# Moving ScalarE's copies and activations by half-states in a kernel of two interleaved layers

## The chip, the cores and the metric

The kernel runs on one core of a Trainium2 chip. The metric is the time in microseconds that the device takes for one launch. A core has a matrix engine (TensorE, here PE, with its weight loads shown as PEld), VectorE (DVE), ScalarE (ACT), GpSimd (POOL) and SyncE (SP), which here only issues transfers. Each engine works through its own queue in order, and they wait for each other through semaphores.

## The reference, cut to what matters

The input `x` is four images of 128 channels by 4096 positions, in fp32. Four layers follow each other; the change touches the first two.

Layer 0 is a selective scan over the positions of an image, with 256 inner channels and 16 states for each:

```python
xt = silu(causal_conv(in_proj(proj(x)))[:256])      # four taps; the other 256 outputs are zg
dt, Bm, Cm = split(xt @ x_proj_w.T)                 # 8 + 16 + 16
delta = softplus(dt @ dt_proj_w.T + dt_proj_b)
for t in positions:                                 # for each of the 16 states n
    h[n] = exp(delta[t] * A[n]) * h[n] + delta[t] * xt[t] * Bm[t, n]
    y[t] = sum_n h[n] * Cm[t, n]
x1 = out_proj((y + xt * D) * silu(zg)) + x
```

Layer 1 takes the group-normed `x1` and makes a hypergraph of the 4096 positions of each image:

```python
incidence = (distance(xf[i], xf[j]) < 16)           # 4096 x 4096 of 0 and 1, symmetric
xe = xf @ W_fc.T + b_fc
edge = (incidence.T @ xe) / degree
vert = (incidence @ edge) / degree
x2 = x1 + silu(batchnorm(vert + xf))
```

Layers 2 and 3 are a linear and a windowed attention, each with a sparse feed-forward layer. They stand in the last 790 us and are not touched.

## The kernel before, in words

**Two streams.** `layer0()` and `layer1()` are generators, and `layers01()` drives them side by side. Image 0 goes through layer 0 alone. Then, for each of the images 0, 1 and 2, layer 1 of image b runs beside layer 0 of image b+1: these are the shared rounds. Layer 1 of image 3 runs alone. Layer 1 of an image needs all of its x1, for the group norm and because every position is compared with every other.

**Layer 0.** An image is cut into eight chunks of T = 512 positions. A chunk takes 16 states, and a state two half-states (h = 0 and 1). A half-state is the unit of time of the whole schedule: one pass of the loop, one `tick`. Its number within a chunk is `u`, from 0 to 31. For each state, `rows` (L292) loads the two rows of B and C from memory on SP's queue, `drive` (L296) multiplies db on POOL, `state` makes two exponentials on ScalarE (L308) into a two-bank PSUM tile `hs` that has two buffers, two scans on VectorE (L314), and one product with C (L325). For image 0, six of the sixteen states have that product (L321) and the carry (L320) on POOL. For later images, POOL adds up groups of eight states instead (L330, L332). TensorE sums the terms (L353).

While one chunk is scanned, the next one is prepared. Its eleven steps are called at the half-states that `slots` names: load, project (eight products into two PSUM tiles `ps_c`, L234), conv (two SiLUs on ScalarE, L241), small (the products `ps_xd`, L247), rows_out (ScalarE's copy xd, L251, and the transfer of it to memory, L253, from which `rows` reads), delta (`ps_d`, L258), parts (L265, L266, twice), exp (L269), ln (L272), and inputs (dl and dx on POOL, L276 and L278). The current chunk's gate is `project_z` (`ps_z`, L361) at u = 9 and `gates` (two SiLUs, L366), and it is used at u = 6 of the following chunk (L371), after which L379 to L382 project, add and store x1.

**Layer 1.** `normed` and `squares` make xn and sq on ScalarE (L491, L486). `tokens` makes xe (products L504, sum on VectorE L508), which ScalarE copies to fp16 (`hi`, L511) and POOL subtracts for a second fp16 part (`lo`, L512). Then follow eight panels of 512 columns of the incidence, from the last to the first. A block is either compared (product L547, comparison on VectorE L550) or, where its mirror image exists, turned by TensorE (L559) and copied by ScalarE (L563). While a panel is made, the one before is multiplied with xs (`edges`, L570, reduced on VectorE L577, scaled and split by L581 to L588). Last comes, for each panel, a row of 1 / degree (`dg` on ScalarE L651, product `ps_r` L671, copied by ScalarE to `rb` L673), 64 products into `ps_v` (L678), and on VectorE the product of the two (`mean`, L686), which frees the bank under `ps_v`.

**What sets the order.** Each yield of `layer1` names its cost in nanoseconds of TensorE time as the writer estimated it; the driver asks for as many yields as keep the shares of both streams equal, about 330 for each half-state. `later(k, f)` puts off a call by k ticks. ScalarE's instructions are chained by hand in the order of the calls: `act()` makes each one follow the one before. For the other engines, the compiler's scheduler orders the instructions by its own cost model, so that a changed call moves instructions on all engines. All matrix products of both streams except `hs` share one PSUM pool, `ps`, of four banks.

Of the kernel before, what the change touches and what calls it, by code (L numbers as in the profile page):

```python
# [12 lines left out]
ALU = mybir.AluOpType  # L13
# [28 lines left out]
class Net:  # L42
# [36 lines left out]
    def layers01(self):  # L79
        nc, tc, a = self.nc, self.tc, self.a  # L80
# [10 lines left out]
        with ExitStack() as ctx:  # L91
# [93 lines left out]
            def follow(i, j):  # L185

                tc.add_manual_dep(
                    i.ins, j.name,
                    mybir.DependencyInfo(mybir.DependencyClass.NoSync, mybir.DependencyReason.DATA),
                    reason="order",  # L190
                )
# [4 lines left out]
            def act(i):  # L196


                if order:
                    follow(i, order[-1])  # L200
                order[:] = [i.ins]
# [5 lines left out]
            def later(k, f):  # L207
                waiting.append((self.tick + k, f))
# [76 lines left out]
            def rows(s, n):  # L285

                bcd = s["bcd"]
                bt = s["bt", n] = bcp.tile([P, 2, T], F32, tag="bt", name="bt")
                ap = bass.AP(
                    tensor=bcd.tensor, offset=bcd[n : n + 1, :].offset, ap=[[0, P], [DS * T, 2], [1, T]]  # L290
                )
                nc.sync.dma_start(bt, ap)  # L292

            def drive(s, n):
                db = s["db", n] = w2.tile([P, 2, T], F32, tag="db", name="db")
                nc.gpsimd.tensor_tensor(db, s["dx"], bc(s["bt", n][:, 0, :], 2), ALU.mult)  # L296
# [61 lines left out]
            def project_z(s):  # L358
                s["pz"] = [ps.tile([P, T], F32, tag="ps", name="ps_z") for h in range(2)]
                for h in range(2):  # L360
                    nc.tensor.matmul(s["pz"][h], wz[:, h, :], s["xt"][:, 3:], start=True, stop=True)  # L361

            def gates(s):
                zs = s["zs"] = late.tile([P, 2, T], F32, tag="zs", name="zs")
                for h in range(2):
                    act(nc.scalar.activation(zs[:, h, :], s["pz"][h], AF.Silu))  # L366

            def gate(s):

                for h in range(2):  # L370
                    nc.vector.tensor_tensor(s["xc"][:, h, :], s["y"][h], s["zs"][:, h, :], ALU.mult)  # L371

            def after(s):

                b, c, xc = s["b"], s["c"], s["xc"]
                x1 = w2.tile([P, T], F32, tag="x1", name="x1", bufs=1)
                po = ps.tile([P, T], F32, tag="ps", name="ps_o")
                for h in range(2):
                    nc.tensor.matmul(po, opT[:, h, :], xc[:, h, :], start=h == 0, stop=h == 1)  # L379
                nc.vector.tensor_tensor(x1, po, s["xt"][:, 3:], ALU.add)  # L380
                nc.vector.bn_stats(self.stats[:, b, c, :], x1)
                nc.scalar.dma_start(self.x1[b][:, c * T : (c + 1) * T], x1)  # L382

            def layer0():

                todo = [before(b, c) for b in range(B) for c in range(NT)]
                for f in todo[0][1]:
                    f()  # L390
                count = len(todo) * DS
                at = lambda i: (todo[i // DS][0], i % DS)

                slots = dict(zip((9, 14, 16, 18, 19, 20, 22, 23, 24, 25, 26), range(11)))

                def steps(k, u):

                    if k > 0:
                        if u == 6:
                            gate(todo[k - 1][0])  # L400
                        if u == 8:
                            after(todo[k - 1][0])
                    if k < len(todo):
                        if u == 9:
                            project_z(todo[k][0])
                        if u == 11:
                            gates(todo[k][0])
                    if k + 1 < len(todo) and u in slots:
                        todo[k + 1][1][slots[u]]()

                for i in range(3):
                    rows(*at(i))
                drive(*at(0))
                for i in range(count):
                    k, n = divmod(i, DS)
                    if i + 3 < count:
                        rows(*at(i + 3))
                    if i + 1 < count:
                        drive(*at(i + 1))
                    state(*at(i), 0)  # L420
                    steps(k, 2 * n)
                    yield
                    state(*at(i), 1)
                    if i > 2:
                        total(*at(i - 3))
                    steps(k, 2 * n + 1)
                    yield
                for i in range(count - 3, count):
                    total(*at(i))
                for u in (6, 8):  # L430
                    steps(len(todo), u)
                yield
# [42 lines left out]
            def layer1(b, rstd, nmr):  # L475
# [18 lines left out]
                def tokens(c, sq):  # L494

                    pc = ps.tile([P, CH], F32, tag="ps", name="ps_hc")
                    for v in range(4):
                        nc.tensor.matmul(
                            pc[:, v : v + 1], sq[:, v * P : (v + 1) * P], self.ones[:, 0:1], start=True, stop=True
                        )  # L500
                    nc.vector.tensor_scalar(hc[:, 4 * c : 4 * c + 4], pc[:, :4], 0.5, -HALF, ALU.mult, ALU.add)
                    pe = ps.tile([P, CH], F32, tag="ps", name="ps_e")
                    for v in range(4):
                        nc.tensor.matmul(  # L504
                            pe[:, v * P : (v + 1) * P], xn[c][:, v * P : (v + 1) * P], wT, start=True, stop=True
                        )
                    xe = tp.tile([P, 4, P], F32, tag="sq", name="xe")
                    nc.vector.tensor_tensor(xe, pe.rearrange("p (i c) -> p i c", c=P), bc(bfc, 4), ALU.add)  # L508
                    hi = xs[:, 4 * c : 4 * c + 4, 0:P]
                    lo = xs[:, 4 * c : 4 * c + 4, P + 1 : 2 * P + 1]  # L510
                    later(2, lambda: act(nc.scalar.copy(hi, xe)))  # L511
                    later(3, lambda: nc.gpsimd.tensor_tensor(lo, xe, hi, ALU.subtract))  # L512

                def row(c, sq=None):

# [144 lines left out]
                for c in range(NCH):  # L660
                    dg = ahead
                    if c < NCH - 1:
                        ahead = diagonals(c + 1)
                    inc = panels[c]
                    if c > 1:
                        inc = tp.tile([P, NB, CH], FP8, tag="inc", name="inc_v")
                        for q in range(4):
                            nc.sync.dma_start(inc[:, 8 * q : 8 * q + 8, :], panels[c][:, 8 * q : 8 * q + 8, :])

                    pr = ps.tile([P, CH], F32, tag="ps", name="ps_r")  # L670
                    nc.tensor.matmul(pr, self.ones, dg.rearrange("p i v -> p (i v)"), start=True, stop=True)  # L671
                    rb = tp.tile([P, CH], F32, tag="rb", name="rb")
                    later(1, lambda rb=rb, pr=pr: act(nc.scalar.copy(rb, pr)))  # L673
                    yield W_DEG
                    pv = ps.tile([P, CH], F32, tag="ps", name="ps_v")
                    for e in range(NB):
                        for k in range(2):
                            nc.tensor.matmul(  # L678
                                pv, es[:, e, k, :], inc[:, e, :],
                                start=e == 0 and k == 0, stop=e == NB - 1 and k == 1,  # L680
                            )
                        if e % 4 == 3:
                            yield W_VERT

                    def mean(c=c, rb=rb, pv=pv):
                        nc.vector.scalar_tensor_tensor(rb, pv, top, rb, ALU.mult, ALU.mult)  # L686
                        nc.gpsimd.tensor_tensor(rb, rb, xn[c], ALU.add)

                    def finish(c=c, rb=rb):

                        follow(nc.vector.bn_stats(stats[:, b, c, :], rb), scans[-1])
                        nc.sync.dma_start(self.hg[b][:, c * CH : (c + 1) * CH], rb)

                    due()
                    later(1, mean)
                    later(6, finish)
# [872 lines left out]
```

## Time and profile before

| | |
|---|---|
| median of three runs | 4049.89 us (4045.8 to 4050.37) |
| profiled execution, its own time | 4054.35 us |
| its span, first to last instruction | 4052.6 us |
| mean granted TensorE clock | 0.929 |
| busy, share of the span | PE 85%, DVE 74%, POOL 61%, ACT 50% |
| layer 0 of image 0 alone | 0 to 597 us |
| shared rounds | 597 to 1328, to 2070, to 2810 us |
| layer 1 of image 3 alone | 2810 to 3262 us |
| the rest of the network | 3262 to 4052 us |

In the lines of the profile, L is a line of the kernel, the arrow points from what is read to what is written, and the brackets at the end hold the idle time of the engine just before an instruction and what ended it. Idle time of an engine that is not the bottleneck costs nothing. The clock is the share of full speed that the throttle granted to TensorE.

### The profile page before, as it was taken

What the parts mean: (1) busy time and instruction counts of PE and PEld (TensorE: products, weight loads), DVE (VectorE), ACT (ScalarE), POOL (GpSimd) and SP (SyncE); (2) the same over time, 40 slices, a digit from 0 to 9 for tenths busy, and PEclk for the clock granted to TensorE, in tenths of its full rate; (3) what the DMA queues carried; (4) which work ended last, traced back from release to release, by engine and by line L of the source; (5) the groups of instructions that cost most, each with busy time, mean ns of one, the idle gap of its engine ahead of it and who ended that gap; (6) DMA issues with size and microseconds to landing.
All of it is one profiled execution on the core that took longest, in us unless ns stands there. A gap on an engine that the chain in (4) does not pass through costs nothing. (4 is left out here: it accounts for less than half of the span.)

```text
span 4052.6 us, 48609 instructions
## 1 busy us (share of the span) xinstructions
PE 3443.5 (85%) x17255; PEld 1930.0 (48%) x17255; DVE 2995.6 (74%) x4628; ACT 2035.6 (50%) x3364; POOL 2460.9 (61%) x1242
## 2 busy tenths in 40 slices
PE   6878768778889788888988888898999979998989
PEld 2333223344544334455433444544566457855864
DVE  5889889999767899976779998665641077665764
ACT  4556555445554545555544455642124068742951
POOL 5999989988779898976989888674000020001300
PEclk8889878999999889999987999998999989999999
DMA  3555544455437444543744555447121420045137
GB/s 103 149 145 156 151 123 127 132 134 156 121 115 233 114 138 131 142 141 91 228 140 128 135 139 150 112 148 242 55 74 49 141 90 12 12 163 200 28 116 296
DMA packets 263845, 532.71 MB, mean 131 GB/s; under 512 B 22794, under 2 KB 25266, under 8 KB 262578
## 3 DMA queue, kind: packets, MB, share of 16 engines
q1 hardware_dynamic: 255666, 519.09, 43.1%
q10 hardware_dynamic: 7936, 10.52, 0.8%
q8 instruction: 136, 2.23, 0.2%
q14 instruction: 107, 0.88, 0.1%
HBM read 451.80 MB, written 77.73 MB: 131 GB/s over the span
## 5 line engine op out<-in xcount | busy, mean ns | idle before, releaser
L296 POOL TENSOR_TENSOR db<-dx,bt 128x1024 f32<-128x1024 f32 x512 | 1203.9, 2355 | 291.2 <-DVE hs L314 159.7
L314 DVE TENSOR_TENSOR_SCAN hs<-hs,carry,db 128x512 f32<-128x512 f32 x812 | 1034.5, 1282 | 293.7 <-ACT hs L308 198.2
L308 ACT ACTIVATE hs<-dl,A 128x512 f32<-128x512 f32 x1024 | 705.9, 692 | 775.6 <-DVE ho L325 725.3
L547 PE MATMUL ps_g<-xn 128*128 128x512 f32 x1152 | 597.6, 646 | 120.6 <-DVE inc L550 86.3
L332 POOL TENSOR_TENSOR ho_s<-ho_s,ho 128x1024 f32<-128x1024 f32 x288 | 678.1, 2355 | 13.3 <-DVE ho L325 7.0
L325 DVE TENSOR_TENSOR ho<-hs,bt 128x1024 f32<-128x1024 f32 x464 | 563.1, 1214 | 1.5
L570 PE MATMUL ps_ed<-xs,inc 128*128 128x258 f16 x4096 | 511.6, 285 | 41.9 <-DVE inc L550 20.3
L570 PEld LDWEIGHTS <-inc 128*128 128x128 fp8e4 x4096 | 416.3, 102 | 160.2 <-issue 87.3
L550 DVE SCALAR_TENSOR_TENSOR inc<-ps_g,hcl,hb 128x512 fp8e4<-128x512 f32 x576 | 419.0, 735 | 32.3 <-PE ps_g L547 18.1
L547 PEld LDWEIGHTS ps_g<-xn 128*128 128x128 f32 x1152 | 210.9, 200 | 439.9 <-DVE inc L550 203.3
L563 ACT CAST inc<-ps_t 128x512 fp8e4<-128x512 f32 x448 | 231.8, 600 | 310.1 <-PE ps_t L559 282.6
L353 PE MATMUL ps_y<-ho,cst 128*128 128x512 f32 x512 | 275.3, 681 | 109.1 <-POOL ho L321 91.8
L678 PE MATMUL ps_v<-inc_v,es 128*128 128x512 fp8e4 x1536 | 344.0, 383 | 8.9 <-DVE rb L686 7.3
L678 PEld LDWEIGHTS <-es 128*128 128x128 f16 x2048 | 202.9, 99 | 277.2 <-issue 53.6
L234 PE MATMUL ps_c<-xt,wc 128*128 128x512 f32 x512 | 236.7, 617 | 2.7 <-DVE inc L550 2.1
L353 PEld LDWEIGHTS ps_y<-ho,cst 128*128 128x128 f32 x512 | 105.6, 215 | 269.7 <-POOL ho L321 122.1
L1238 POOL CAST b1h<-b 128x512 bf16<-128x512 f32 x2 | 1.4, 680 | 302.5 <-DMA b<-in_L_ffn_weight 302.5
L586 POOL TENSOR_TENSOR ed<-ed,rdeg 128x512 f32<-128x512 f32 x32 | 33.3, 1040 | 245.9 <-DVE rdeg L582 245.9
L314 DVE TENSOR_TENSOR_SCAN hs<-hs,db 128x512 f32<-128x512 f32 x116 | 141.3, 1224 | 49.4 <-POOL db L296 42.8
L577 DVE TENSOR_REDUCE ed<-ps_ed 128x129 f32<-128x258 f32 x128 | 52.9, 413 | 157.6 <-PE ps_ed L570 157.6
L234 PEld LDWEIGHTS ps_c<-xt,wc 128*128 128x128 f32 x512 | 100.5, 199 | 127.8 <-issue 116.1
L1474 POOL MEMSET ob<- 128x256 f32 x4 | 1.2, 312 | 261.7 <-PE ps_t L1417 261.7
(317 smaller groups left out, 5448.5 us busy)
## 6 DMA issues: line engine op xcount, KB each, us to landing
bt<-bcd SPq DMA_DIRECT2D x512, 512.0 KB, 5.0
w<-in_L_ffn_weight SPq DMA_DIRECT2D x64, 1024.0 KB, 11.4
inc<-inc SPq DMA_DIRECT2D x192, 256.0 KB, 2.3
inc_v<-inc SPq DMA_DIRECT2D x96, 512.0 KB, 6.3
strip<-inc SPq DMA_DIRECT2D x84, 256.0 KB, 2.9
x<-x ACTq DMA_DIRECT2D x32, 256.0 KB, 5.4
xn<-x SPq DMA_DIRECT2D x32, 256.0 KB, 6.2
hg<-rb SPq DMA_DIRECT2D x32, 256.0 KB, 2.5
```

The costliest lines, as they stand in the source:

```text
L234: nc.tensor.matmul(s["ps"][h], wc[:, h, j, :], xt[:, j : j + T], start=j == 0, stop=j == 3)
L296: nc.gpsimd.tensor_tensor(db, s["dx"], bc(s["bt", n][:, 0, :], 2), ALU.mult)
L308: act(nc.scalar.activation(hs[:, k, :], s["dl"][:, k, :], AF.Exp, scale=A[:, k, n : n + 1]))
L314: i = nc.vector.tensor_tensor_scan(to[:, h, :], hs[:, h, :], db[:, h, :], init, ALU.mult, ALU.add)
L325: nc.vector.tensor_tensor(ho, hs, ct, ALU.mult)
L332: nc.gpsimd.tensor_tensor(s["sum", n // G], s["sum", n // G], ho, ALU.add)
L353: nc.tensor.matmul(s["y"][h], self.ident, t[:, h, :], start=False, stop=n == DS - 1 and k == len(terms) - 1,)
L547: nc.tensor.matmul(pq, xn[v // 4][:, v % 4 * P : (v % 4 + 1) * P], xn[c], start=True, stop=True)
L550: nc.vector.scalar_tensor_tensor(inc[:, v, :], pq, hc[:, v : v + 1], hb, ALU.subtract, ALU.is_gt, saturate=False)
L563: later(1, lambda: act(nc.scalar.copy(inc[:, v, :], pt, saturate=False)))
L570: nc.tensor.matmul(pe[:, : 2 * P + 2], inc[:, v, i * P : (i + 1) * P], xs[:, v, :], start=v == 0, stop=v == NB - 1,)
L678: nc.tensor.matmul(pv, es[:, e, k, :], inc[:, e, :], start=e == 0 and k == 0, stop=e == NB - 1 and k == 1,)
```

## The change

Five places move. `slots` calls project one half-state earlier (14 to 13) and everything from rows_out on one half-state later, so that conv stands three half-states behind project instead of two, and rows_out two behind small instead of one; delta and the steps after it keep their distances. `gates` stands three half-states behind `project_z` instead of two. The copy of xe stands three ticks behind it instead of two, and POOL's subtraction goes one tick later with it. The copy of the row of 1 / degree stands three ticks behind its product instead of one.

```diff
@@ layer0
-                slots = dict(zip((9, 14, 16, 18, 19, 20, 22, 23, 24, 25, 26), range(11)))
+                slots = dict(zip((9, 13, 16, 18, 20, 21, 23, 24, 25, 26, 27), range(11)))
...
                         if u == 9:
                             project_z(todo[k][0])
-                        if u == 11:
+                        if u == 12:
                             gates(todo[k][0])
@@ layer1, tokens
-                    later(2, lambda: act(nc.scalar.copy(hi, xe)))
-                    later(3, lambda: nc.gpsimd.tensor_tensor(lo, xe, hi, ALU.subtract))
+                    later(3, lambda: act(nc.scalar.copy(hi, xe)))
+                    later(4, lambda: nc.gpsimd.tensor_tensor(lo, xe, hi, ALU.subtract))
@@ layer1, rows of 1 / degree
                     rb = tp.tile([P, CH], F32, tag="rb", name="rb")
-                    later(1, lambda rb=rb, pr=pr: act(nc.scalar.copy(rb, pr)))
+                    later(3, lambda rb=rb, pr=pr: act(nc.scalar.copy(rb, pr)))
```

## The prediction

> **What bounds the kernel now.** I read the page's table of engines first. It names no bound: PE 85%, DVE 74%, POOL 61% are means over unlike stages. So I asked for busy time by stretch. One shared round (layer 0 of image b+1 beside layer 1 of image b) is 597 to 1328 us; the rounds from 1328 and 2070 repeat it wait for wait.
>
> ```profile
> 0.00:597.00 597.00, 449.76 (x910) 182.50 (x911) 480.32 (x540) 335.47 (x445) 498.34 (x259) 0.87 0.48 138
> 597.00:1000.00 403.00, 329.19 (x1256) 163.93 (x1255) 379.79 (x486) 208.38 (x297) 361.13 (x164) 0.91 0.49 135
> 1000.00:1140.00 140.00, 116.47 (x775) 77.24 (x774) 100.51 (x124) 84.89 (x138) 100.26 (x46) 0.92 0.45 123
> 1140.00:1180.00 40.00, 31.95 (x163) 17.79 (x161) 20.74 (x26) 17.01 (x29) 21.23 (x12) 0.87 0.18 57
> 1180.00:1325.00 145.00, 140.26 (x562) 61.48 (x560) 108.73 (x117) 67.70 (x107) 132.78 (x61) 0.99 0.72 218
> ```
>
> After start and length the columns are busy us of PE, PE's weight loads, DVE, ACT, POOL, then granted TensorE clock. While panels are compared (597 to 1000) DVE is the bound: 379.79 of 403 us. While panels are mostly turned (1000 to 1140) nobody is above 84% and the engines wait for each other in order. From 1180 to 1325 PE is the bound (140.26 of 145), POOL next (132.78). In the first 597 us (layer 0 alone) it is POOL: 498.34 us busy, and half of its 99 us of idleness lies in the setup at the start.
>
> Next the waits of that round, since the change moves only what ScalarE waits for:
>
> ```profile
> DVE hs L314 <- ACT hs L308: 67.9, 21, 9.4
> ACT inc L563 <- PE ps_t L559: 50.1, 17, 5.9
> ...
> PE ps_g L547 <- DVE inc L550: 30.3, 32, 3.3
> ...
> ACT xd L251 <- PE ps_xd L247: 21.6, 8, 6.4
> ACT rb L673 <- PE ps_r L671: 20.9, 6, 10.3
> ...
> ACT xc L241 <- PE ps_c L234: 14.0, 4, 7.8
> ```
>
> Each line is a waiter, its releaser, us in all, times, longest. The change addresses xd, rb and xc: 56.5 us of ScalarE's waiting a round. What counts is the DVE idleness that they cause, part of the 67.9. In time order, 25 us of that 67.9 stands from 1000 to 1140 behind the turned panels' copies (L563), which stay where they are (one half-state behind); before 1000 only 9.2, also behind L563. The other 34 stands from 1140 on. On ScalarE's timeline, with what each waited for in brackets:
>
> ```profile
> 1144.17 0.69 ACT L241 ACTIVATE xc<-ps_c,vec 128x512 f32<-128x512 f32 x1 [7.80 <-PE ps_c L234]
> ...
> 1168.35 0.62 ACT L587 CAST es<-ed 128x512 f16<-128x512 f32 x1 [9.86 <-POOL ed L586]
> ...
> 1227.48 0.59 ACT L673 COPY rb<-ps_r 128x512 f32<-128x512 f32 x1 [10.29 <-PE ps_r L671]
> ```
>
> and on PE's, its one long gap there:
>
> ```profile
> 1170.20 2.07 PE L671 MATMUL ps_r<-dg,ones 128*128 128x512 f32 x2 [8.05 <-ACT dg L651]
> ```
>
> Between them xd (L251) waited 5.04 us until 1156.6. But there PE is the bound: DVE's gaps are mostly slack. Hence the gain is small.
>
> **The change part by part.** No instruction is added or removed but three activation table loads (227 against 224 in the built programs). Everything else is place in a queue. I compared the built instruction orders, which hold no times.
>
> Gates, xd, delta, parts, exp, ln and inputs move one half-state later; conv and small stay; the chunk's projection is asked for one half-state earlier, but on PE it stays within 3.5 us of its old place, so the 7.80 us wait at L241 stays. ACT's bcd DMA moves with xd; its reader, the bt load on SP, is issued six half-states later instead of seven, of about 2.9 us each (731 us / 256), and bt lands in 5.0 us: covered. If bcd were later than that, SP would hold every load behind it.
>
> *First stage.* The POOL order changes at each chunk end: the carry copy (L320) and ho (L321) come before dl (L276) instead of after.
>
> ```profile
> 219.98 2.34 POOL L276 TENSOR_TENSOR dl<-dl,sp 128x1024 f32<-128x1024 f32 x1 [0.42 <-ACT sp L272]
> ...
> 241.63 0.19 POOL L320 COPY carry<-ho 128x2 f32<-128x2 f32 x1 [0.61 <-DVE ho L314]
> ```
>
> ```profile
> 222.72 2.62 DVE L314 TENSOR_TENSOR_SCAN hs<-hs,carry,db 128x512 f32<-128x512 f32 x2 [2.71 <-POOL carry L320]
> ```
>
> DVE's 2.71 us goes, but POOL is the bound, so only POOL's own idleness counts: the 0.42 (dl starts 4.7 us later, after two 2.35 us operations, while ln is one half-state later) and about 0.3 of the 0.61: DVE starts the next chunk some 2 us earlier, but is then held by db, late next at 2.35 us each. 0.7 us by 8 chunks: -5.6. Bounds: 0, and -2 a chunk if DVE's lead were kept.
>
> *Compare and turn (597 to 1140), three times.* DVE has no gap behind an addressed wait here; what hides it is that ScalarE runs two states ahead. Gain 0. The cost is PSUM: ps has four banks; z and c keep two each for three half-states instead of two, xd one for two instead of one: 5 more bank-half-states of 128 in a chunk. DVE waited for PE's products about 17 us a round in all (inc 3.8, ed 9.8, hb 3.6). Bounds: 0, and +5 a round if these waits grow with the banks that layer 0 holds (about 16 to 21 of 128, +30%). Nearest row: inc's own 3.8, 30% of it 1.1. Taken: +1.3, +4 in all. Moving xe's copy and POOL's subtraction one half-state later shortens the time until xe's buffer is wanted (3.2 and 3.6 us at the tightest); xs waits are on ACT only. Counted at 0, bound +2 a round.
>
> A rule speaks against this step. The Trainium skill, "Perfetto Trace Analysis", section Identifying Performance Opportunities, says that the same bubble repeating on the engine that should be saturated can mean that no PSUM is free for the next tile. By that, PE's 30.3 us before ps_g, released by DVE, would grow by a third and cost up to +10 a round, +30. The rows differ: DVE, the bound, waits 3.8 us for these very products. I use the rows.
>
> Table loads: ACT_TABLE_LOAD is 1283 ns in the rows and the next instruction starts 10 to 20 ns later, so three cost 3.9 us. "ScalarE: Activation LUTs", What ACT_TABLE_LOAD costs, gives about 2.66 us per switch with its drain: 8 us. No row here shows that drain. ACT is busy 50%; counted 0.
>
> *End of the edges (1140 to 1180), three times.* Now: last edge product ends at 1160.2, ps_d follows (1.98), then PE idles 8.05 until dg. The last scans before the closing reduce (L577) start at 1158.6, because ScalarE stood at xd before the exps of that state. In the new order those exps come before xd: they can start at 1151.5, DVE's scans at 1155.3 instead of 1158.6. Reduce and reciprocal end near 1161.5, POOL's ho_s (2.34) and ed (1.04) near 1164.4, es and dg (0.62 + 1.26) near 1166.3. Late next is POOL. But ps_d now comes after ps_r, so PE idles 6.1 instead of 8.05: -1.9 a round, -5.8.
>
> *Products with the edges (1180 to 1325).* rb three half-states behind ps_r instead of one. ScalarE no longer stands 10.29 us at L673; PE had only 4.0 us of idleness in this stretch, 3.37 of it for DVE rb L686 freeing a bank. DVE runs ahead, POOL allows no more than its idleness. L686 stands one state (two scans of 1.28 and a product of 1.21, 3.8 us) later in DVE's order for five of the first seven panels. With DVE 5 us further ahead it comes out earlier: -2 in two rounds, -4. In the last stage (layer 1 alone) the same copy has 14 us of ps_v to hide in: 0.
>
> *Between rounds.* PE idles 7.25 us at 1325 for sq (L486) of the next image. In the new order the chunk projection (7.03 us) stands ahead of that wait. DVE only idles 0.97 + 1.23 for what this delays: -2 at two crossings, -4.
>
> Sum: -5.6 + 4 - 5.8 - 4 - 4 = -15.4. The profiled execution took 4054.35 us (span 4052.6 and 1.75 around it), so 4039; it is 0.11% above the median 4049.89, against which I forecast 4034.5.
>
> **The rivals.** A: no change (4042 to 4058). The waits only move: ScalarE stands at L563 instead, and PE decides. For it: DVE's gaps lie where PE is the bound. Against: the 0.42, the 8.05 and the order at the crossing. Time 4050, with the gains of the crossing and first stage eaten by PSUM.
>
> B: slower, by the bank under ps_v. A panel's bank is freed by L686, now a state later in DVE's order. Where PE comes to the next bank with none free it idles; it did 3.37 us once a round already. Three of the seven panel ends have no slack: PE waited for L686 at two (0.27 and 3.37), and at another ps_y's two banks were wanted 0.4 us after it. If DVE gains nothing, since POOL (132.78 of 145) holds it, each costs 3.6: 3 by 3.6 by 3 = +32. With the first stage (-5.6), the crossings (-4) and PSUM (+4), +27: 4077. With half of that, 4063. It decides once DVE is less than 3.6 us further ahead of PE at those ends.
>
> C: a larger gain: DVE's gaps at xc, xd, rb (6.64, 3.01, 5.67, 3.52, 3.46: 22.3 a round) are all worth time: -67, 3983. Against: PE busy 97% there.
>
> **How the numbers follow.** Forecast (faster by about 15) 0.5, A 0.2, B 0.25, C 0.05. The line between a change and none is 0.2%, 8 us, about what a measurement of this kernel tells apart. Faster 0.53, same 0.2, slower 0.27. The forecast's own range is 4020 to 4046. To hold 8 in 10 the range takes in A and most of B, 4012 to 4068.
>
> **What would show it.** Right: POOL's order at chunk ends without the 0.42; PE's gap before the first ps_r at 6 instead of 8.05; L673's wait for ps_r in shared rounds below 8 us in place of 20.9; ps_c in the gap at a round's start. Wrong: PE idle before ps_v in front of L686 for more than 5 us a round (B), more than 10 us of DVE waiting for ps_g a round (PSUM), or xe waiting for xs on POOL.

## The result: slower by 0.59%, and the profile after

The changed kernel took 4071.06 us (median of four runs, 4069.93 to 4074.56), the kernel before 4047.85 us on the same chip (four runs, 4042.37 to 4050.37). The ratio is 1.0059, 95% interval 1.0046 to 1.0072. The profiled execution of the changed kernel took 4071.98 us, its span is 4070.2 us, and the granted clock is 0.927 against 0.929. The clock is not what costs the time: the gates moved alone lose 17.8 us at a clock of 0.932. The forecast was 4034.5.

DVE's addition that makes x1 (L380, one a chunk) starts in the changed kernel 1.4 us earlier in chunk 0 of image 0, and then later by 1.9, 4.7, 8.7, 11.7, 14.3, 18.8 and 19.5 us. The last mean (L686) of the shared rounds is late by 19.3. So the loss has formed before the first shared round starts, and the three rounds together come out even. They do so because a gain and a loss meet in them: up to each round's first `ps_r` the three rounds together take 1779.4 us for 1799.7 before, and from there to the round's last mean 470.2 us for 450.1. (All figures of this kind are of one execution each. Where the instruction order is the same, two of them differ by some 3 us over the rounds.)

The first stage of the changed kernel (stretch, length, then busy us of PE, weight loads, DVE, ACT and POOL, then granted clock):

```profile
0.00:617.00 617.00, 459.66 (x933) 185.23 (x933) 482.38 (x541) 338.22 (x448) 495.97 (x259) 0.88 0.46 133
```

It is 20 us longer (617 for 597), while POOL, its bound, has the same work (495.97 for 498.34). The products with the edges in the first shared round, from the first `ps_r` to the last mean, before and after:

```profile
1170.20:1325.30 155.10, 150.30 (x596) 65.65 (x596) 114.33 (x123) 76.71 (x122) 135.77 (x62) 0.98 0.68 204
```

```profile
1183.00:1345.90 162.90, 153.39 (x601) 67.00 (x602) 114.99 (x122) 73.94 (x119) 135.78 (x62) 0.96 0.64 194
```

They are 7.8 us longer, and PE idles 9.5 us in them for 4.8.

**The first stage.** Between the first and the last x1 of image 0 lie seven chunks. Before:

```profile
126.00:558.50 432.50, 346.73 (x694) 136.49 (x692) 373.56 (x382) 257.74 (x342) 390.35 (x202) 0.89 0.52 150
```

After:

```profile
124.60:578.00 453.40, 353.01 (x693) 138.73 (x691) 375.06 (x383) 257.65 (x342) 390.37 (x202) 0.89 0.48 142
```

POOL is busy 390.35 and 390.37 us, so its idleness went from 42.15 to 63.03 us: 3.0 us a chunk more, which is the whole growth of the chunk (61.8 to 64.8 us). Now, who makes it wait? Waits of the same stretch, before (waiter, releaser, us in all, times, longest):

```profile
PE ps_y L353 <- POOL ho L321: 75.5, 23, 5.9
...
POOL carry L320 <- DVE ho L314: 27.2, 17, 4.0
...
DVE hs L314 <- POOL carry L320: 16.3, 6, 2.7
...
POOL dl L276 <- ACT sp L272: 3.8, 7, 1.2
```

And after:

```profile
PE ps_y L353 <- POOL ho L321: 95.4, 26, 6.1
POOL carry L320 <- DVE ho L314: 48.3, 22, 5.0
...
ACT xc L241 <- PE ps_c L234: 35.0, 14, 2.8
...
DVE ho L314 <- ACT hs L308: 26.9, 13, 4.3
```

The two waits that the prediction saw go have left the list: `dl` on `sp` and DVE on POOL's carry. Two others have grown from almost nothing: ScalarE waits 35.0 us for `ps_c` (1.5 before), and DVE 26.9 us for ScalarE's exponentials (0.5 before). POOL's wait for DVE grew by 21.1 us. On the timeline of the changed kernel one can follow the chain. PE:

```profile
264.73 3.61 PE L353 MATMUL ps_y<-ho,cst 128*128 128x512 f32 x4 [3.84 <-POOL ho L321]
268.18 7.03 PE L234 MATMUL ps_c<-xt,wc 128*128 128x512 f32 x16
```

ScalarE:

```profile
267.75 1.28 ACT L241 ACT_TABLE_LOAD   x1
271.81 0.69 ACT L241 ACTIVATE xc<-ps_c,vec 128x512 f32<-128x512 f32 x1 [2.78 <-PE ps_c L234]
275.25 0.69 ACT L241 ACTIVATE xc<-ps_c,vec 128x512 f32<-128x512 f32 x1 [2.75 <-PE ps_c L234]
275.95 1.28 ACT L308 ACT_TABLE_LOAD   x1
277.25 2.75 ACT L308 ACTIVATE hs<-dl,A 128x512 f32<-128x512 f32 x4
```

DVE, then POOL:

```profile
278.75 2.46 DVE L314 TENSOR_TENSOR_SCAN ho<-hs,carry,db 128x512 f32<-128x512 f32 x2 [4.22 <-ACT hs L308]
```

```profile
281.27 0.19 POOL L320 COPY carry<-ho 128x2 f32<-128x2 f32 x1 [4.91 <-DVE ho L314]
```

PE takes its queue in order. In front of `ps_c` now stand products of `ps_y` whose operand POOL makes, and PE waits 3.84 us for it. So `ps_c` starts late, ScalarE stands twice at `xc` with the table for SiLU loaded, the exponentials behind come late, DVE's scan with them, and POOL, the bound, idles 4.91 us. Before, the same chunk had on PE

```profile
255.29 1.88 PE L353 MATMUL ps_y<-ho,cst 128*128 128x512 f32 x4
257.00 7.03 PE L234 MATMUL ps_c<-xt,wc 128*128 128x512 f32 x16
263.87 2.31 PE L353 MATMUL ps_y<-ho,cst 128*128 128x512 f32 x5
```

with no wait, and ScalarE's two SiLUs ran at 264.14 without one. The gates are what put it there: between `ps_z` and the `ps_c` of chunks 2 to 7 of image 0, PE has four products of `ps_y` in every kernel below whose gates stay at u = 11 there, and eight in the change and in the kernel with the gates alone moved. The gates free the two banks of `ps_z`, and they come one half-state later. That the held banks are the scheduler's reason is a reading of the order; the place on PE is what the experiments below test.

**The shared rounds.** PE's gap before the first `ps_r` and its start of the next round, changed kernel:

```profile
1183.01 2.08 PE L671 MATMUL ps_r<-dg,ones 128*128 128x512 f32 x2 [6.01 <-ACT dg L651]
...
1345.74 7.03 PE L234 MATMUL ps_c<-xt,wc 128*128 128x512 f32 x16
1353.38 1.12 PE L520 MATMUL ps_hb<-sq,ones 128*128 128x512 f32 x2 [0.61 <-ACT sq L486]
```

The 8.05 became 6.01, and the 7.25 before `ps_hb` became 0.61, as forecast. ScalarE's wait for `ps_r`, 20.9 us in the first round, is down to

```profile
ACT rb L673 <- PE ps_r L671: 3.2, 3, 1.5
```

(The rounds do not repeat this wait as the prediction took it: 20.9, 11.5 and 41.6 us before, 3.2, 3.2 and 37.7 after.) But inside the edge products PE now waits:

```profile
1222.79 1.80 PE L678 MATMUL ps_v<-inc_v,es 128*128 128x512 fp8e4 x6 [2.27 <-DMA inc_v<-inc]
...
1326.94 8.36 PE L678 MATMUL ps_v<-inc_v,es 128*128 128x512 fp8e4 x32 [6.42 <-DMA bt<-bcd]
```

The first label is right. The product waits for a part of the third panel's incidence, which is loaded again from memory. On SP's queue that load stands behind the store of the first panel's result (`hg`, which SP holds until POOL has added to the mean) and behind a `bt` load for layer 0:

```profile
1214.16 0.33 SPq L692 DMA_DIRECT2D hg<-rb  x1
1214.59 0.39 SPq L292 DMA_DIRECT2D bt<-bcd  x1
1215.03 2.70 SPq L668 DMA_DIRECT2D inc_v<-inc  x3
```

The part landed at 1222.75, 7.7 us after its issue, and PE starts at 1222.79. Before, the load stood directly behind the store and landed after 4.4 us. The label of the second line is wrong, since that product reads no `bt`. DVE's timeline shows what it waits for:

```profile
1325.01 1.21 DVE L325 TENSOR_TENSOR ho<-hs,bt 128x1024 f32<-128x1024 f32 x1
1326.14 0.74 DVE L686 SCALAR_TENSOR_TENSOR rb<-ps_v,top,rb 128x512 f32<-128x512 f32 x1
```

DVE's mean, which frees the bank, ends at 1326.88 and PE starts at 1326.94. Before, the same gap bore DVE's name:

```profile
1305.88 2.41 PE L678 MATMUL ps_v<-inc_v,es 128*128 128x512 fp8e4 x7 [3.37 <-DVE rb L686]
```

The longer wait for the bank is rival B's mechanism in rival B's place; the wait for the load is not in the prediction. Both follow the later `rb`, and the gaps before `ps_v` in the three rounds have grown by 6.1 us for the one and 6.1 for the other.

### The profile page after: what moved, and what is told of

The parts are those of the page before. It is cut to its first block, busy times and chain, and to the rows that moved or that the text cites. A ratio compares the mean times of both kernels' runs of the same rounds, so it can differ in the third digit from the quotient of the medians.

```text
span 4070.2 us, 48577 instructions
## 1 busy us (share of the span) xinstructions
PE 3456.8 (85%) x17255; PEld 1931.6 (47%) x17255; DVE 2981.3 (73%) x4628; ACT 2037.6 (50%) x3367; POOL 2461.0 (60%) x1242
## 5 line engine op out<-in xcount | busy, mean ns | idle before, releaser
L353 PE MATMUL ps_y<-ho,cst 128*128 128x512 f32 x512 | 287.9, 708 | 123.7 <-POOL ho L321 110.1
L678 PE MATMUL ps_v<-inc_v,es 128*128 128x512 fp8e4 x1536 | 344.5, 383 | 20.9 <-DMA bt<-bcd 13.1
L678 PEld LDWEIGHTS <-es 128*128 128x128 f16 x2048 | 202.0, 99 | 289.5 <-issue 65.4
## 6 DMA issues: line engine op xcount, KB each, us to landing
w<-in_L_ffn_weight SPq DMA_DIRECT2D x64, 1024.0 KB, 11.7
```

What stands on the lines that cost most here:

```text
L353: nc.tensor.matmul(s["y"][h], self.ident, t[:, h, :], start=False, stop=n == DS - 1 and k == len(terms) - 1,)
L678: nc.tensor.matmul(pv, es[:, e, k, :], inc[:, e, :], start=e == 0 and k == 0, stop=e == NB - 1 and k == 1,)
```

## The experiments

Each kernel ran 5 to 21 times (the change 4) beside the kernel before. Kernels timed together share the runs of before, whose median was 4051.07, 4049.74 and 4049.83 us in the three groups. "Us from before" is the ratio less one, by 4050. The intervals are 3 to 6 us to each side, so that a difference of two kernels is uncertain by some 4 to 8 us. Kernels with the order edge have their lines some 1 to 4 further down (L678 becomes L682, L686 becomes L690).

| kernel | median us | ratio, 95% interval | us from before |
|---|---|---|---|
| the change | 4071.06 | 1.0059 (1.0046 to 1.0072) | +23.9 |
| gates alone | 4065.97 | 1.0044 (1.0031 to 1.0056) | +17.8 |
| change, order edge in image 0 | 4045.66 | 0.9988 (0.9981 to 0.9994) | -4.9 |
| change, image 0 as before | 4049.94 | 0.9997 (0.9989 to 1.0005) | -1.2 |
| change, gates put back | 4062.64 | 1.0031 (1.0019 to 1.0042) | +12.6 |
| rb alone | 4071.01 | 1.0058 (1.0046 to 1.0071) | +23.5 |
| change, edge, rb put back | 4024.52 | 0.9942 (0.9930 to 0.9955) | -23.5 |
| gates alone, edge | 4046.54 | 0.9995 (0.9987 to 1.0003) | -2.0 |
| projection and rows alone | 4042.47 | 0.9985 (0.9976 to 0.9993) | -6.1 |
| change, edge, rb and xe put back | 4024.93 | 0.9944 (0.9931 to 0.9958) | -22.7 |
| change, gates and rb put back | 4043.29 | 0.9984 (0.9978 to 0.9991) | -6.5 |
| xe alone | 4055.97 | 1.0017 (1.0010 to 1.0023) | +6.9 |
| change, edge, rb at two | 4034.99 | 0.9964 (0.9951 to 0.9976) | -14.6 |

**Gates alone.**

```diff
-                        if u == 11:
+                        if u == 12:
```

> The kernel before with only the gates moved from half-state 11 to 12. Theory (the first stage is where the time is lost, because the chunk projection ps_c now stands on PE behind the state-4 products of ps_y, which wait for POOL's ho): in this order ps_c stands behind those products in image 0 too, so a chunk of the first stage takes about 65 us instead of 62 and the program about 4067 (+19). Rival (the projection's half-state, 14 to 13, or the rows' order makes the loss): within 4 us of before, 4048.

4065.97 us. In its trace the x1 of chunk 7 is 18.2 us late and a chunk takes 64.7 us, as in the changed kernel. ScalarE's wait for `ps_c` and POOL's for the scan are there too:

```profile
POOL carry L320 <- DVE ho L314: 45.1, 17, 5.0
ACT xc L241 <- PE ps_c L234: 33.4, 14, 2.9
```

The projection's new half-state and the rows are not needed for the loss.

**The change with one order edge.** In image 0, the products of `ps_y` are told to follow the last projection that was asked for. Nothing else differs from the change, so the gates are still late.

```diff
-                            nc.tensor.matmul(
+                            i = nc.tensor.matmul(
                                 s["ps"][h], wc[:, h, j, :], xt[:, j : j + T], start=j == 0, stop=j == 3
                             )
+                    projected[:] = [i.ins]
...
-                        nc.tensor.matmul(
+                        i = nc.tensor.matmul(
                             s["y"][h], self.ident, t[:, h, :],
...
+                        if s["b"] == 0:
+                            follow(i, projected[-1])
```

> The changed kernel with one order edge: in image 0 the products of ps_y stand on PE behind the chunk projection that was asked for before them. Theory (the place of ps_c on PE is the loss): PE's wait for ho ahead of ps_c in the first stage goes, its chunks are back at about 62 us, and the program at about 4050 (-20 against the change). Rival (the moved gates themselves, later by a half-state on ScalarE, lengthen the chunk): 4065 to 4071, chunks of about 65 us.

4045.66 us, within the theory's reach. A chunk takes 61.8 us, and in the same seven chunks the waits read

```profile
POOL carry L322 <- DVE ho L316: 28.5, 23, 3.9
...
PE ps_c L235 <- ACT zs L370: 19.7, 7, 4.3
...
ACT xc L243 <- PE ps_c L235: 6.2, 7, 2.2
```

PE now waits 19.7 us for the gates, so the late gates do cost PE something, but PE is not the bound here. ScalarE's 35.0 is 6.2 and POOL is where it was. The place of `ps_c` on PE is therefore the cause, and the late gates by themselves are not. The edge is worth 28.8 us (23.9 + 4.9). By the traces, whose ends differ by 27.9, 21.7 of that lies in image 0 (578.0 against 556.3 for the last x1), 3.8 in the second and third round, and the rest behind the shared rounds; what makes the last two isn't known. The busy times of the seven chunks:

```profile
123.90:556.30 432.40, 343.45 (x694) 136.43 (x693) 374.74 (x382) 256.57 (x341) 389.39 (x202) 0.91 0.51 149
```

POOL idles 43.0 us, as much as before (42.15).

**The change with image 0 as before.** Old `slots` and old gate as long as layer 0 runs alone.

```diff
+                slots0 = dict(zip((9, 14, 16, 18, 19, 20, 22, 23, 24, 25, 26), range(11)))
...
-                        if u == 12:
+                        if u == (11 if k < NT else 12):
...
-                    if k + 1 < len(todo) and u in slots:
-                        todo[k + 1][1][slots[u]]()
+                    own = slots0 if k < NT else slots
+                    if k + 1 < len(todo) and u in own:
+                        todo[k + 1][1][own[u]]()
```

> The change, but with the old half-states of projection, gates and rows while image 0 runs alone. Theory (all of the loss is in the first stage, the shared rounds together about even): 4045 to 4053, with the first xe of round 1 where it was before. Rival (the shared rounds lose by the bank under ps_v and make it up only because they start late): 4058 or more.

4049.94 us: no change. So the shared rounds and the last stage are together even. The difference of 3.7 us to the run with the edge is within the uncertainty of two runs, and seven chunks take 432.0 us in this kernel, with the old order, and 432.5 with the new half-states and the edge: a gain in the first stage isn't shown.

**The change with the gates put back.**

```diff
-                        if u == 12:
+                        if u == 11:
```

> The change with the gates alone put back to half-state 11. Theory: ps_c stays ahead of the state-4 products in the first stage, chunks of about 62 us; the rest of the change is worth within 6 us of nothing, 4042 to 4054. Rival (the rest of the change costs by itself in the first stage): 4060 or more.

4062.64 us: the first half of the theory held (chunk 7's x1 at 558.6 against 558.5), the second did not. The time is lost in the shared rounds, 4.8 us in the first, 7.3 in the second. In the first it stands 4.7 us ahead of before at the first `ps_r` and 4.8 behind at the last mean. So the loss is in the products with the edges, where `rb` was moved. From the first `ps_r` to the last mean the three rounds take 473.4 us in this kernel, 450.1 before.

**rb alone.**

```diff
-                    later(1, lambda rb=rb, pr=pr: act(nc.scalar.copy(rb, pr)))
+                    later(3, lambda rb=rb, pr=pr: act(nc.scalar.copy(rb, pr)))
```

> The kernel before with only the copy rb of a row of degrees three half-states behind its product instead of one. Theory (the mean that frees the bank of ps_v comes later on DVE, and PE waits for the bank): first stage unchanged, each of the three shared rounds 2 to 5 us longer in the products with the edges, the program +6 to +14: 4057 to 4065. The forecast's own step said 2 us shorter in two rounds: 4046.

4071.01 us, worse than the theory said and as slow as the whole change. The first stage is as before (+1.4 us at chunk 7; the four kernels with the old order of image 0 are within 2.2 us there). PE's gap at the seventh panel is now 7.00 us, and DVE's mean again ends just as it closes:

```profile
1312.05 8.23 PE L678 MATMUL ps_v<-inc_v,es 128*128 128x512 fp8e4 x29 [7.00 <-DMA bt<-bcd]
```

```profile
1311.25 0.74 DVE L686 SCALAR_TENSOR_TENSOR rb<-ps_v,top,rb 128x512 f32<-128x512 f32 x1
```

In the three rounds PE's gaps of over 0.5 us before `ps_v` sum to 26.4 us, against 7.9 before. Of the growth of 18.5 us, 7.3 is at the seventh panel and 11.2 before `ps_v` of the third, where PE waits 3.6 to 4.9 us a round for the load of `inc_v`. In the kernel with the gates put back, the gap at the seventh panel carries the name that the times point to:

```profile
1310.10 1.44 PE L678 MATMUL ps_v<-inc_v,es 128*128 128x512 fp8e4 x3 [6.42 <-DVE rb L686]
```

**The change with the edge, rb put back.** The last diff in the other direction, on top of the order edge.

> The change with the order edge in image 0, and with rb back at one half-state. Theory (rb's lag hands back, in the products with the edges, the lead of 10 us that the kernel has at the first ps_r): PE's gaps before ps_v at 3.4 us or less instead of 2.2 and 6.4, and the program 4 to 12 us under the run with the edge alone: 4034 to 4042. Rival (POOL or PE hold that stretch whatever rb does): within 3 us of the run with the edge alone, 4043 to 4049.

4024.52 us, well below the theory's lower end: faster than before by 0.58%, and by 18.6 us than the edge alone (each against the kernel before). PE's timeline, at the first `ps_r`, the seventh panel's end and the next round's start:

```profile
1158.31 2.07 PE L675 MATMUL ps_r<-dg,ones 128*128 128x512 f32 x2 [6.01 <-ACT dg L655]
...
1294.61 9.86 PE L682 MATMUL ps_v<-inc_v,es 128*128 128x512 fp8e4 x32 [3.26 <-DVE rb L690]
...
1314.93 7.03 PE L235 MATMUL ps_c<-xt,wc 128*128 128x512 f32 x16
1322.66 1.12 PE L524 MATMUL ps_hb<-sq,ones 128*128 128x512 f32 x2 [0.70 <-ACT sq L490]
```

It keeps the short gaps (6.01 and 0.70) and has only the old one before `ps_v`. On SP the load of the third panel stands directly behind the store again, and its first part lands 4.7 us after its issue:

```profile
1190.03 0.33 SPq L696 DMA_DIRECT2D hg<-rb  x1
1190.41 1.39 SPq L672 DMA_DIRECT2D inc_v<-inc  x3
```

The length of the stretch from the first `ps_r` to the last mean follows `rb` alone, whatever else is moved: for the three rounds together it is 447.7 to 453.5 us in the eight kernels with `rb` one half-state behind (before among them), 460.2 in the one with two, and 470.2 to 473.4 in the five with three. How much of the 20 us is the bank and how much the load isn't separated by a run. And ScalarE waits in it for `ps_r` longer than before (20.9):

```profile
ACT rb L677 <- PE ps_r L675: 23.8, 6, 10.9
```

The fastest kernel of all has the wait that the change takes away; the change, one of the two slowest, has 3.2 us of it in the same round.

**Gates alone, with the edge.** The first diff and the order edge.

> The kernel before with only the gates moved to half-state 12, and the order edge in image 0. Theory (the later gates are the part of the change that gains, once ps_c stays in its place: -2 in the first stage, and -7 in the shared rounds as in the run with the gates alone): 4038 to 4044. Rival (the shared rounds gained there only because they started 18 us late): 4046 to 4051.

4046.54 us; here the rival was right. The interval takes in no change. (The edge was not timed on the kernel before, where `ps_c` stands in that place without it.) PE's gap before the first `ps_r` stays at 8.05.

**Projection and rows alone.** The new `slots`, nothing else.

> The kernel before with only the new half-states of projection and rows; gates, xe and rb stay. Theory (with the gates put back, the changed kernel lost about 3 us a round, all of it to rb's lag): within 4 us of before, 4044 to 4052. Rival (rows pushed behind gates that stay are the loss): 4056 to 4062.

4042.47 us, a little better than the theory. The gap before the first `ps_r` is 6.00 and that before `ps_hb` 0.6, so both gaps close with the new `slots` alone; which of the two half-states in them, project's or that of rows_out, closes which isn't separated.

**The change with the edge, rb and xe put back**, that is gates, projection and rows alone:

> The run with the order edge and rb at one half-state, with the lags of xe's copy and subtraction put back too, so that gates, projection and rows alone are moved. Theory (gates and rows gain singly about 3 and 7 us, so xe's lag must carry some 15 of the 25 us): about 4039. Rival (the later copies work together, and xe's lag costs, as DVE waits 1.67 us for xs on POOL at the start of a round): 4018 to 4025.

4024.93 us. The rival was right: gates (-2.0) and rows (-6.1) give -22.7 together. No effect of xe's lag is seen beside it (-23.5 with it).

**The change with gates and rb put back.**

> The change without the gates' move and without rb's lag: projection, rows and xe moved. Theory (rb's lag costs 21 us wherever it stands, and the run with the gates put back lost 12): 4040, 9 us under before. Rival (later gates are what the rest needs: with the gates put back there is nothing to gain): 4046 to 4052.

4043.29 us, between the two expectations and nearer to the first. Against the kernel with only the gates put back, it says that rb's lag costs 19.1 us (12.6 + 6.5); rb alone said 23.5, and the pair with the edge 18.6.

**xe alone.**

> The kernel before with only xe's copy and subtraction one half-state later. Forecast's step: 0, at most +6. Theory of single parts (xe carries what gates and rows do not): -15, 4035. Theory of parts that work together: within 4 us of before.

4055.97 us, a small loss, a little over the bound of +6 that the forecast's step named. On top of gates and rows none is seen.

**The change with the edge, rb at two.**

```diff
-                    later(3, lambda rb=rb, pr=pr: act(nc.scalar.copy(rb, pr)))
+                    later(2, lambda rb=rb, pr=pr: act(nc.scalar.copy(rb, pr)))
```

> The change with the order edge, rb two half-states behind instead of three. Theory (the cost is the place of the mean on DVE, not the copy's own lateness): the time follows how many panels' means stand a scan or more later, so between 4024 (lag one) and 4046 (lag three). Rival (one half-state more is free, since DVE waits for POOL in that stretch anyway): 4022 to 4027.

4034.99 us: one half-state costs 8.9 us, the second 9.7. In DVE's order of the first round three means stand two scans later than with lag one; with lag three it is five. The way in which it costs is instructive, for its gaps before `ps_v` are no longer than in the kernel with lag one. Counted from the first `ps_r`, the second panel's mean comes 4.5 us later on DVE, and what waits is not the next panel but layer 0's own product, which shares the four banks:

```profile
1203.42 1.12 PE L340 MATMUL ps_y<-xc,dD 128*128 128x512 f32 x2 [3.06 <-DVE rb L690]
```

In the kernel with lag one the same product stands at 1198.45 without a wait. This is the third place that rival B named ("ps_y's two banks were wanted 0.4 us after it"). In the three rounds these waits before `ps_y` are 9.2 us. With lag three and the edge they are only 2.0; there the seventh panel's gap of 6.43 us and the 2.2 us at the third, for the load, stand in their place.

## Why the prediction was wrong

All four signs named for a right forecast appeared: POOL's order without the 0.42, the gap of 6.01, ScalarE's wait for `ps_r` at 3.2 us (in two of the three rounds), and `ps_c` in the gap at a round's start. So did two of the signs against it: PE idle for more than 5 us in front of L686 (6.42), and xe waiting for xs on POOL (1.7 us a round). The steps took place, but the sum had two terms wrong: it put the place of `ps_c` on PE at nothing, and it gave the later `rb` a gain.

Its sum against the runs. Each measured figure is the difference of two kernels that differ in that part alone (the first against before, with the order edge), uncertain by some 6 us:

| part | predicted us | measured us |
|---|---|---|
| gates, projection and rows, `ps_c` in its place | -11.4 (-5.6 + 4 - 5.8 - 4) | -22.7 |
| xe one half-state later | 0 | -0.8 |
| rb two half-states later | -4 | +18.6 |
| `ps_c` behind products that wait for POOL | not in it | +28.8 |
| sum | -15.4 | +23.9 |

The same by stages, from the traces, in us from before (the trace of before is of an execution 4.5 us above its median):

| stage | predicted | the change | gates, projection and rows, with the edge |
|---|---|---|---|
| first stage, to the last x1 | -5.6 | +19.5 | -2.4 |
| three rounds, each to its first `ps_r` | -5.8 (-4 + 4 - 5.8) | -20.3 | -24.1 |
| three rounds, each from there to its last mean | -4 (by the later `rb`) | +20.1 | -0.8 (`rb` as before) |
| after the rounds | 0 | -1.7 | 0.0 |

*First stage: the step that failed most.* The prediction saw two waits go (POOL's 0.42 and DVE's 2.71), and they went. Its own term, -5.6, did not come: POOL idles 42.15 us in seven chunks before and 43.0 with the new half-states and the edge. Worse, it took PE's order for unchanged: "on PE it stays within 3.5 us of its old place, so the 7.80 us wait at L241 stays". That was read from the wait at L241 in a shared round. In the first stage `ps_c` went behind products that need POOL's ho, so the few us became a wait on the bound itself, in each of the chunks. Its bounds for the stage, 0 and -2 a chunk, held no loss at all; the measured one was about +3 a chunk.

*Products with the edges: the sign was wrong.* The step knew that L686 stands a state later for five of the first seven panels. It let "DVE 5 us further ahead" bring it out earlier. That lead did not come: from the first `ps_r` to the last mean of the first round, DVE waits for ScalarE as long as before. Before and after:

```profile
DVE hs L314 <- ACT hs L308: 24.2, 6, 9.4
```

```profile
DVE hs L314 <- ACT hs L308: 23.7, 5, 7.6
```

Rival B had the mechanism and the condition under which it decides, and its price of 3.6 us a place is close to the growth from 3.37 to 6.42 us at the seventh panel, and, with lag two, to the 3.06 us at `ps_y`. It had not seen the load that comes late behind the store, which makes as much of the new gaps before `ps_v`. Its 32 us for three rounds stands against 18.6 to 23.5 measured. Its time of 4077 comes near the 4071 in part by luck, since it had the first stage as a gain.

*End of the edges: right.* The gap before the first `ps_r` was to be 6.1 and is 6.01, in every kernel with the new rows, and 8.05 in every one without.

*Between rounds: right in its mechanism, but it bought nothing.* `ps_c` fills the gap as forecast, and the first comparison of the second round comes 12.4 us early with the rows alone, where the round's last mean was 4.7 early. After 18 comparisons the lead is 5.6 us, and after 36 it is 4.5: all of the gain is handed back. In the kernel with edge and old rb, where the lead is 10.2 us at the last mean, 19.3 at the first comparison and 7.6 after 36, DVE waits in between for POOL's db:

```profile
1369.16 1.23 DVE L316 TENSOR_TENSOR_SCAN hs<-hs,db 128x512 f32<-128x512 f32 x1 [3.45 <-POOL db L298]
```

The -4 came to about nothing. That POOL sets the pace again there, so that what PE gained is not kept, is a reading of such waits and not tested.

*Compare and turn: no cost was found in the change.* The +4 for the banks didn't come, nor the +30 by the rule of the Trainium skill ("Perfetto Trace Analysis", Identifying Performance Opportunities: a bubble that repeats on the engine that should be saturated can mean that no PSUM is free for the next tile). In the first round of the changed kernel PE waits for DVE before `ps_g`

```profile
PE ps_g L547 <- DVE inc L550: 28.2, 25, 3.5
```

for 28.2 us, against 30.3 before, DVE waits 1.0 us for these products (3.8 before), and over the stretch the kernel loses nothing: it is late by 21.3 us at the comparison that stood at 711 us before, and by 16.8 at the edge reduction that stood at 1137. The rule was about the right resource, though: a bank's late release cost its price at the panels' ends, and, if the held banks are what moved `ps_c`, in image 0.

*What was not foreseen on the good side.* Gates and rows moved together gain 22.7 us, twice the sum of the predicted terms and nearly three times the sum of the two moved singly (8.1). By the traces the three rounds of the kernel with gates, projection and rows are shorter than before by 5.7, 6.8 and 12.4 us (cut at the last x1 of image 0 and at each round's last mean); with gates alone and the edge by 2.1, -0.5 and 7.9, with projection and rows alone by 0.2, -0.5 and 6.3. So the pair is 9.4 us ahead of the two singles in these stretches, and 14.6 by the times. Where they differ is in the comparing and turning: between the 61st and the 133rd comparison of a round (784 to 1044 us before), DVE, for the three rounds together, is idle 88.3 us before, 87.3 with the gates alone, 100.4 with the rows alone, and 86.9 with both. So rows without the gates' move cost DVE there some 4 us a round, which the move takes away, although it holds two banks longer. Why stays open.

## What to carry to other kernels

When one operation is put off, look at what its buffer's later release does to the order of the in-order engine that wants the buffer next, stage by stage: a product that slips behind one which waits for the bound turns a harmless delay into a wait of the bound. A wait on an engine that isn't the bound (20.9 us of ScalarE in the first round here) need not be a gain to be had; and before a copy is put off, ask what stands behind it on the way to freeing a PSUM bank, because the last link, here a product on VectorE, may be pushed back by whole scans, and what stands behind its result in a queue of transfers comes late with it. Test the parts of such a change apart and together: gates, projection and rows were worth 22.7 us together, xe nothing that could be seen, rb cost 19, and the gates needed an order edge in one stage; with rb put back and the edge added, the kernel took 4024.52 us for 4049.74 before.

## What the profile showed that I had not expected

The name that the profile gives to the end of a wait can be wrong or right in neighbouring lines, and the times tell which. PE's 6.42 us bore the name of the `bt` load, which that product does not read; it ended within 0.06 us of DVE's mean, and the same gap in the first round of the kernels with image 0 as before and with the gates put back (6.42 us in both) names DVE. The 2.27 us bore the name of the `inc_v` load, and that load did land within 0.04 us of the product's start. Of the chip itself the runs showed nothing unexpected: the granted clock was 0.927 to 0.935 in the profiled executions of all these kernels and doesn't order their times.
